# A four-layer graph network on one core: the preamble recorded in the plan, and the last six groups levelled, with all their steps through DRAM

## The chip, the core and the metric

The kernel runs on one core of a Trainium2 chip. The metric is device time in microseconds, from the first to the last instruction of the core; the time before is the median of three runs, 1416.56 us (1415.75 to 1422.14). The engines are named as in the profile: PE is TensorE (matmuls), PEld its weight loads, DVE VectorE, ACT ScalarE, POOL GpSimd, SP SyncE (here the issuer of most DMAs).

## The reference

`x` has 64 graphs of 256 nodes with 128 features, `adj` is one 256 x 256 matrix for all graphs, and everything is float32. Each of four layers adds its result to `x` and normalises over the features. Cut to what is computed:

```python
def layernorm(x): return (x - mean(x)) / sqrt(var(x) + 1e-5)        # over the 128 features

# layer 0: powers of adj, twice the same matrix; weight (128, 128, 7)
parts = [x, adj@x, adj@adj@x, adj@adj@adj@x, adj@x, adj@adj@x, adj@adj@adj@x]
x = layernorm(x + einsum('bnik,iok->bno', stack(parts), w0))
# layer 1
x = layernorm(x + adj @ (x @ w1) + b1)
# layer 2: A_hat = adj + I, d = rowsum(A_hat)**-0.5
x = layernorm(x + (d[:, None] * A_hat * d[None, :]) @ x @ W2.T + b2)
# layer 3: five gated steps with in_matrix = out_matrix = adj
h = x
for _ in range(5):
    m = adj @ h;  av = concat([m, m]);  u3 = h @ u3_w.T + u3_b
    z = sigmoid(av @ w3_w.T + w3_b + u3)
    r = sigmoid(av @ w4_w.T + w4_b + u3)
    hv = tanh(av @ w5_w.T + w5_b + (r * h) @ u5_w.T + u5_b)
    h = (1 - z) * h + z * hv
x = layernorm(x + h)
```

## The kernel before

Two graphs make a group: 2 x 256 nodes x 128 features lie as one 128 x 512 float32 tile, and 32 groups pass through the layers. The weights are folded in advance (`w34T` is the third gate weight less the fourth, so that `pr` serves first for r and then for z). A preamble makes the constants, in the program order in which it is written. Then each group is recorded as a list of operations, with an engine, a cost, what it reads and writes and a rank (the group's number); a list scheduler (`Plan.order`) settles the order of instructions of every engine and the buffer of every value. At most six groups are active.

The preamble:

```python
    a_nat = const.tile([P, T, N], F32, name="a_nat")
    nc.sync.dma_start(a_nat, adj.rearrange("(t p) m -> p t m", p=P))
    ...
    for mt in range(T):
        pt = bank(f"at_{mt}")
        for nt in range(T):
            nc.tensor.transpose(pt[:, nt * P:(nt + 1) * P], a_nat[:, nt, mt * P:(mt + 1) * P], ident)
        nc.vector.tensor_copy(aT[:, mt, :], pt[:, :N])
    ...                                   # aTp: the rows of aT in another order, by four DMAs
    for mt in range(T):
        pt = bank(f"apow_{mt}")
        for kt in range(T):
            mm(pt[:, :N], a_nat[:, kt, mt * P:(mt + 1) * P], aT[:, kt, :], kt == 0, kt == T - 1)
        nc.vector.tensor_copy(a2T[:, mt, :], pt[:, :N])
    ...                                   # anT: normalised adjacency, with deg, dinv (POOL) and ahat
    w0_raw = const.tile([P, C, K0], F32, name="w0_raw")
    nc.scalar.dma_start(w0_raw, w0)
    ...                                   # w1s, b1s, b2s
    w34 = halves("w3T", w3_w)
    nc.vector.tensor_sub(w34, w34, w4b)
    w4T = transposed("w4T", w4b)          # one TensorE transpose and one DVE copy each
    ...                                   # w34T, w5T, u3T, u5T; biases zb, rb, hb, two column DMAs each
```

A group's load, first propagation, and its five steps. `propagate` multiplies with the adjacency into `pmq`, `pm` or `pmg` and copies the result with ACT. A step needs `h` in node layout for the propagation and `hT` in feature layout for everything else. The first 30 groups get `h` from `hT` by a DVE transpose of 32 x 32 blocks, a store to DRAM and two rearranging reads (`packed`); the last two (TAIL = 2) by four TensorE transposes (`pth`) and an ACT copy.

```python
            x_ = self.val("x", "x")
            plan.add("SP", 450, 2700, g, lambda: nc.sync.dma_start(nat(x_), view(x, g)), [], [x_], self.load_gate)
            if g < HEAD:                                   # HEAD = 2
                xT = self.copied("xT", self.transposes("x", x_))
            else:
                xT = self.brought("xT", self.turned("x", x_, ...))     # DVE transpose (tx), DRAM, four reads
            qT = self.propagate("q", x_, a2)
            ...                                            # layers 0, 1 and 2
            if g < G - TAIL:
                hT = self.brought("hT", self.turned("h", h, ...))
                outs = by_block
            else:
                pT = self.transposes("h", h)
                ...
            for s in range(STEPS):
                m = self.propagate(f"g{s}", h, ats, ins, outs)
                pr = self.val("bank", f"pr{s}")
                self.product(pr, u3T, hT, True, False)
                self.product(pr, w4T, m, False, True)
                r = self.gate_(f"r{s}", pr, AF.Sigmoid, rb)
                rh = self.tensor(f"rh{s}", OP.mult, r, hT)
                ph = self.val("bank", f"ph{s}")
                self.product(ph, w5T, m, True, False)
                self.product(pr, w34T, m, False, True, shared=True)
                z = self.gate_(f"z{s}", pr, AF.Sigmoid, zb)
                self.product(ph, u5T, rh, False, True)
                hv = self.gate_(f"hv{s}", ph, AF.Tanh, hb)
                d = self.tensor(f"d{s}", OP.subtract, hv, hT)
                e = self.tensor(f"e{s}", OP.mult, z, d)
                hT = self.tensor(f"hT{s}", OP.add, hT, e)
                if g < G - TAIL:
                    if s < STEPS - 1:
                        h, ats, ins = self.packed(f"h{s}", hT), a1p, pair_of
                else:
                    pT = self.transposes(f"h{s}", hT)
                    if s < STEPS - 1:
                        h = self.copied(f"h{s}", pT)
            ...                                            # residual (s), statistics (st, mv, ve, rs), y, output
```

A float32 product of 512 columns shows as two TensorE passes in the profile (x2), a propagation as eight.

Of the kernel before, what the change touches and what calls it, by code (L numbers as in the profile page):

```python
# [13 lines left out]
P = 128  # L14
# [3 lines left out]
TAIL = 2  # L18
STEPS = 5
EPS = 1e-5  # L20
# [3 lines left out]
class Val:  # L24

# [16 lines left out]
class Plan:  # L42
# [29 lines left out]
    def order(self):  # L72
        free = {}
        pool = {k: [(0.0, i) for i in range(n)] for k, n in self.slots.items()}
        left = {op: len(op.deps) for op in self.ops}
        after = {op: [] for op in self.ops}
# [9 lines left out]
        while any(ready.values()):  # L86
            best = None
            for e, waiting in ready.items():
                t0 = free.get(e, 0.0)
                pick = None  # L90
                for at, op in waiting:
                    need = {}
                    for v in op.vals:
                        if v.slot is None:
                            need[v.kind] = need.get(v.kind, 0) + 1
                    short = False
                    for k, n in need.items():
                        if len(pool[k]) < n:
                            short = True
                            break  # L100
                        at = max(at, sorted(pool[k])[n - 1][0])
                    if short:
                        continue
                    key = (max(at, t0), op.rank, op.seq)
                    if pick is None or key < pick[0]:
                        pick = (key, op)
# [7 lines left out]
            for v in op.vals:  # L114
# [30 lines left out]
def kernel(  # L145
# [39 lines left out]
    prep = ctx.enter_context(tc.tile_pool(name="prep", bufs=2))  # L185
    setup = ExitStack()
    psum = setup.enter_context(tc.tile_pool(name="psum", bufs=BANKS, space=bass.MemoryType.PSUM))

    def bank(name):
        return psum.tile([P, 512], F32, tag="bank", name=name)  # L190

    def mm(o, lhsT, rhs, start, stop, shared=False):
        nc.tensor.matmul(o, lhsT, rhs, start=start, stop=stop, skip_group_check=shared)  # L193


    ident = const.tile([P, P], F32, name="ident")
    make_identity(nc, ident)
    a_nat = const.tile([P, T, N], F32, name="a_nat")
    nc.sync.dma_start(a_nat, adj.rearrange("(t p) m -> p t m", p=P))
# [4 lines left out]
    aT = const.tile([P, T, N], F32, name="aT")  # L204
    a2T = const.tile([P, T, N], F32, name="a2T")
    for mt in range(T):
        pt = bank(f"at_{mt}")
        for nt in range(T):
            nc.tensor.transpose(pt[:, nt * P:(nt + 1) * P], a_nat[:, nt, mt * P:(mt + 1) * P], ident)
        nc.vector.tensor_copy(aT[:, mt, :], pt[:, :N])  # L210

    aTp = const.tile([P, T, N], F32, name="aTp")
    for k in range(4):
        nc.sync.dma_start(aTp.rearrange("(i k) t n -> k i t n", k=4)[k], aT[32 * k:32 * (k + 1)])
    for mt in range(T):
        pt = bank(f"apow_{mt}")
        for kt in range(T):
            mm(pt[:, :N], a_nat[:, kt, mt * P:(mt + 1) * P], aT[:, kt, :], kt == 0, kt == T - 1)
        nc.vector.tensor_copy(a2T[:, mt, :], pt[:, :N])


    ahat = const.tile([P, T, N], F32, name="ahat")
    nc.vector.tensor_copy(ahat, a_nat)
    for t in range(T):
        diag = ahat[:, t, t * P:(t + 1) * P]
        nc.vector.tensor_add(diag, diag, ident)
    deg = const.tile([P, T], F32, name="deg")
    nc.vector.reduce_sum(deg, ahat, axis=AX.X)
    dinv = const.tile([P, T], F32, name="dinv")
    nc.gpsimd.tensor_tensor(dinv, deg, half[:, :T], op=OP.pow)  # L230
    for t in range(T):
        nc.vector.tensor_scalar(ahat[:, t, :], ahat[:, t, :], dinv[:, t:t + 1], None, op0=OP.mult)
    anT = const.tile([P, T, N], F32, name="anT")
    for mt in range(T):
        pt = bank(f"an_{mt}")
        for nt in range(T):
            nc.tensor.transpose(pt[:, nt * P:(nt + 1) * P], ahat[:, nt, mt * P:(mt + 1) * P], ident)
        nc.vector.tensor_scalar(anT[:, mt, :], pt[:, :N], dinv[:, mt:mt + 1], None, op0=OP.mult)
# [3 lines left out]
    w0_raw = const.tile([P, C, K0], F32, name="w0_raw")  # L242
    nc.scalar.dma_start(w0_raw, w0)

    w0s = const.tile([P, 4, C], F32, name="w0s")
    nc.vector.tensor_add(w0s[:, 0, :], w0_raw[:, :, 0], ident)
    for k in (1, 2, 3):
        nc.vector.tensor_add(w0s[:, k, :], w0_raw[:, :, k], w0_raw[:, :, k + 3])
    w1s = const.tile([P, C], F32, name="w1s")
    nc.scalar.dma_start(w1s, w1)  # L250
    b1s = const.tile([P, C], F32, name="b1s")
    nc.scalar.dma_start(b1s, bass.AP(tensor=b1.tensor, offset=b1.offset, ap=[[0, P], [1, C]]))
    b2s = const.tile([P, C], F32, name="b2s")
    nc.scalar.dma_start(b2s, bass.AP(tensor=b2.tensor, offset=b2.offset, ap=[[0, P], [1, C]]))

    def transposed(name, src):
        pt = bank(f"pt_{name}")
        nc.tensor.transpose(pt[:, :P], src, ident)
        t = const.tile([P, P], F32, name=name)
        nc.vector.tensor_copy(t, pt[:, :P])  # L260
        return t

    def loaded(name, src, shape):
        t = prep.tile(shape, F32, tag=f"raw{shape[1]}", name=f"raw_{name}")
        nc.scalar.dma_start(t, src)
        return t

    def halves(name, src):
        raw = loaded(name, src, [P, 2 * C])
        both = const.tile([P, C], F32, name=f"both_{name}")  # L270
        nc.vector.tensor_add(both, raw[:, :C], raw[:, C:])
        return both

    def bias_sum(name, a, b):
        raw = prep.tile([P, 2], F32, tag="rawb", name=f"raw_{name}")
        nc.scalar.dma_start(raw[:, 0:1], a.rearrange("(p o) -> p o", o=1))
        nc.scalar.dma_start(raw[:, 1:2], b.rearrange("(p o) -> p o", o=1))
        t = const.tile([P, 1], F32, name=name)
        nc.vector.tensor_add(t, raw[:, 0:1], raw[:, 1:2])
        return t  # L280

    w2T = transposed("w2T", loaded("w2T", w2, [P, C]))


    w4b = halves("w4T", w4_w)
    w34 = halves("w3T", w3_w)
    nc.vector.tensor_sub(w34, w34, w4b)
    w4T = transposed("w4T", w4b)
    w34T = transposed("w34T", w34)
    w5T = transposed("w5T", halves("w5T", w5_w))  # L290
    u3T = transposed("u3T", loaded("u3T", u3_w, [P, C]))
    u5T = transposed("u5T", loaded("u5T", u5_w, [P, C]))
    zb = bias_sum("zb", w3_b, u3_b)
    rb = bias_sum("rb", w4_b, u3_b)
    hb = bias_sum("hb", w5_b, u5_b)


    SHAPES = {"bank": [P, 512], "x": [P, 512], "w": [P, 512], "dram": [P, 512], "st": [P, Q * 6], "mv": [P, Q * 2],
              "ve": [P, Q], "rs": [P, Q]}
    slots = {"bank": BANKS, "x": ACTIVE + 3, "w": 58, "dram": 16, "st": 8, "mv": 8, "ve": 8, "rs": 8}  # L300
    plan = Plan(slots)
# [29 lines left out]
    class Group:  # L331
        def __init__(self, g):
            self.g, self.first, self.last = g, None, None
            self.gate = self.load_gate = ()

# [3 lines left out]
        def add(self, engine, cost, lag, run, reads=(), writes=()):  # L339
            after = () if self.first else self.gate  # L340
            op = plan.add(engine, cost, lag, self.g, run, reads, writes, after)
# [54 lines left out]
        def propagate(self, tag, h, aTs, ins=None, outs=None):  # L396
# [3 lines left out]
            def run():  # L400
                o, a = (outs or plain)(ps), ins or tile_of
                for b in range(NB):
                    for kt in range(T):
                        mm(o[b], a(h, b * T + kt), aTs[kt], kt == 0, kt == T - 1)

            self.pe(pe_cost(N, NB * T), run, [h], [ps])
# [49 lines left out]
        def product(self, ps, w, rhs, start, stop, shared=False):  # L456
            self.pe(pe_cost(512), lambda: mm(ps.ap, w, rhs.ap, start, stop, shared), [rhs], [ps])

        def gate_(self, name, ps, func, bias):
            t = self.val("w", name)  # L460
            self.act(lambda: nc.scalar.activation(t.ap, ps.ap, func, bias=bias, scale=1.0), [ps], [t],  # L461
# [3 lines left out]
        def tensor(self, name, op, a, b):  # L465
            t = self.val("w", name)
            self.dve(dve_cost(512), lambda: nc.vector.tensor_tensor(t.ap, a.ap, b.ap, op=op), [a, b], [t])  # L467
            return t

        def record(self):  # L470
# [10 lines left out]
            qT = self.propagate("q", x_, a2)  # L481
# [3 lines left out]
            for t in range(T):  # L485
# [3 lines left out]
                def first(p=p, t=t):  # L489
                    for b in range(NB):  # L490
                        o, n0 = p.ap[:, b * 2 * C:(b + 1) * 2 * C], b * N + t * P
                        mm(o, xT.ap[:, n0:n0 + P] if g < HEAD else by_node(xT)[:, b * T + t, :], w0s[:, 0:2, :], b == 0, True, shared=True)
                        mm(o, qT.ap[:, n0:n0 + P], w0s[:, 2:4, :], False, True, shared=True)
# [4 lines left out]
                self.pe(pe_cost(2 * C, 2 * NB), first, [xT, qT], [p])  # L498
                self.act(moved, [p], [v], act_cost(256))
            for t in range(T):  # L500

                def second(p=py[t], t=t):
                    for kt in range(T):
                        mm(four(p)[:, :, 0, :], aT[:, kt, t * P:(t + 1) * P], parts(v)[:, kt],
# [6 lines left out]
                self.pe(pe_cost(NB * C, T), second, [v], [py[t]])  # L511
# [4 lines left out]
            for tag, ats, w, bias in (("1", a1, w1s, b1s), ("2", an, w2T, b2s)):  # L516
                yb = self.val("w", "yb" + tag)

                def biased(yb=yb, y=y, bias=bias):
                    nc.gpsimd.tensor_tensor(nat(yb), nat(y), bias[:, None, :].to_broadcast([P, Q, C]),  # L520
                                            op=OP.add)

                self.add("POOL", 1290, 100, biased, [y], [yb])
# [3 lines left out]
                def weight(py=py, m=m, w=w):  # L527
                    for q in range(Q):
                        mm(py.ap[:, q * P:(q + 1) * P], m.ap[:, q * P:(q + 1) * P], w, True, True)

                self.pe(pe_cost(P, Q), weight, [m], [py])
# [4 lines left out]
            outs = None  # L536
            if g < G - TAIL:
# [96 lines left out]
```

## Time and profile before

| | |
|---|---|
| time, median of 3 | 1416.56 us (1415.75 to 1422.14) |
| span of the profiled run | 1415.3 us, 16464 instructions |
| granted TensorE clock, mean | 0.995 |
| PE / PEld / DVE / ACT / POOL busy | 97% / 65% / 68% / 36% / 16% |
| chain that ended last | PE 95%, DVE 2%, DMA 1%, ACT 1% |
| DMA traffic | 129.76 MB, 92 GB/s over the span |

The page gives busy time by engine, then 40 slices of the span, each digit a tenth of busy time, then the chain of work that ended last. Queries of the trace add timelines, waits and busy time by chosen stretch. A busy TensorE in it isn't TensorE at its peak, because its passes overlap and their ends are modelled: what is exact is when each starts. Idle time of an engine that isn't the bound costs nothing.

### The profile page before, as it was taken

The page shows a single profiled execution, that of the slowest core. Times are in us where ns is not written, and L with a number is a line of the kernel's source. Part 1 is how long each engine was busy: PE and PEld are TensorE (multiplying, and loading weights), DVE is VectorE, ACT ScalarE, POOL GpSimd, SP SyncE. Part 2 cuts the span into 40 slices and gives each one's busy share as a digit, 9 for nine tenths or more (in the row PEclk, how much of TensorE's full clock was granted, in tenths as well). Part 3 has the DMA queues.
Part 4 walks back from the last instruction along what each step waited for, and adds up shares of the span by engine and source line. Part 5 has one row for each costly group of instructions (what it writes and reads, how often), then busy time and mean ns, then how long its engine had stood idle before and what let it go on. Part 6 is the DMA issues. An engine that isn't in the chain of part 4 may idle for free.

```text
span 1415.3 us, 16464 instructions
## 1 busy us (share of the span) xinstructions
PE 1376.4 (97%) x5006; PEld 925.0 (65%) x5006; DVE 967.8 (68%) x2706; ACT 511.8 (36%) x812; POOL 224.5 (16%) x199
## 2 busy tenths in 40 slices
PE   5999999999999999999999999999999999999994
PEld 4866666667766676656666666676666766766552
DVE  3666577758775787857867666775777676676654
ACT  1233433343343323343333333334333344333442
POOL 0411011101210031201202111210121111121000
PEclk9999999999999999999999999999999999999998
DMA  5022343323333332324323333232433233322101
GB/s 169 16 60 80 92 128 111 95 76 105 105 104 91 100 108 76 111 82 135 98 82 104 97 100 114 88 110 75 118 104 98 82 112 90 97 82 67 53 23 30
DMA packets 245448, 129.76 MB, mean 92 GB/s; under 512 B 137968, under 2 KB 218224, under 8 KB 245360
## 3 DMA queue, kind: packets, MB, share of 16 engines
q1 hardware_dynamic: 243056, 127.46, 30.5%
q10 hardware_dynamic: 2304, 1.25, 0.4%
q8 instruction: 40, 0.66, 0.2%
q14 instruction: 48, 0.39, 0.1%
HBM read 64.95 MB, written 63.44 MB: 91 GB/s over the span
## 4 chain that ended last, share of the span: by engine, by line
PE 95%; DVE 2%; DMA 1%; ACT 1%; issue 0%; POOLq 0%; POOL 0%; SPq 0%; DVEq 0%; ACTq 0%
PE pr L193 29%; PE pmg L193 19%; PE ph L193 19%; PE py L193 16%; PE pm L193 8%; PE pmq L193 4%; DMA x<-in_x_dram 1%; PE pth L414 0%; DVE e L467 0%; DVE d L467 0%; DVE hT L467 0%; PE apow L193 0%; DVE y L390 0%; ACT hv L461 0%; DVE st L365 0%
## 5 line engine op out<-in xcount | busy, mean ns | idle before, releaser
L376 POOL TENSOR_TENSOR rs<-ve,half 128x4 f32<-128x4 f32 x128 | 134.1, 1050 | 1080.9 <-DVE ve L370 1076.2
L467 DVE TENSOR_TENSOR d<-hv,hT 128x512 f32<-128x512 f32 x160 | 112.6, 705 | 189.4 <-ACT hv L461 186.4
L467 DVE TENSOR_TENSOR rh<-r,hT 128x512 f32<-128x512 f32 x160 | 115.0, 719 | 166.7 <-ACT r L461 162.7
L193 PE MATMUL pmg<-aTp,h 128*128 128x256 f32 x960 | 225.0, 379 | 0.0
L193 PEld LDWEIGHTS pmg<-aTp,h 128*128 128x128 f32 x960 | 187.8, 196 | 42.8 <-issue 19.7
L357 ACT COPY mg<-pmg 128x512 f32<-128x512 f32 x160 | 93.8, 586 | 234.8 <-PE pmg L193 218.5
L461 ACT ACTIVATE z<-pr,zb 128x512 f32<-128x512 f32 x160 | 109.9, 688 | 168.9 <-PE pr L193 160.0
L390 DVE TENSOR_SCALAR y<-s,mv,rs 128x128 f32<-128x128 f32 x512 | 143.9, 345 | 36.7 <-POOL rs L376 36.3
L193 PE MATMUL pr<-mg,w4T 128*128 128x512 f32 x320 | 163.3, 593 | 1.4 <-ACT mg L357 1.4
L193 PE MATMUL pr<-mg,w34T 128*128 128x512 f32 x320 | 162.7, 594 | 1.7 <-ACT r L461 1.6
L193 PE MATMUL ph<-rh,u5T 128*128 128x512 f32 x320 | 162.2, 593 | 0.3 <-DVE rh L467 0.3
L193 PE MATMUL ph<-mg,w5T 128*128 128x512 f32 x320 | 162.4, 592 | 0.0
L193 PE MATMUL pr<-hT,u3T 128*128 128x512 f32 x320 | 161.5, 595 | 0.5 <-DVE hT L467 0.5
L461 ACT ACTIVATE r<-pr,rb 128x512 f32<-128x512 f32 x160 | 110.0, 688 | 128.5 <-PE pr L193 118.3
L461 ACT ACTIVATE hv<-ph,hb 128x512 f32<-128x512 f32 x160 | 110.0, 687 | 42.7 <-PE ph L193 41.5
L467 DVE TENSOR_TENSOR e<-z,d 128x512 f32<-128x512 f32 x160 | 111.7, 702 | 2.2
L467 DVE TENSOR_TENSOR hT<-hT,e 128x512 f32<-128x512 f32 x160 | 109.4, 687 | 2.4
L365 DVE BATCH_NORM_STATS2 st<-s 128x6 f32<-128x128 f32 x512 | 109.5, 277 | 0.7
L193 PEld LDWEIGHTS ph<-rh,u5T 128*128 128x128 f32 x320 | 60.5, 190 | 72.9 <-issue 62.0
L193 PEld LDWEIGHTS ph<-mg,w5T 128*128 128x128 f32 x320 | 60.5, 190 | 70.5 <-issue 54.8
L193 PEld LDWEIGHTS pr<-mg,w34T 128*128 128x128 f32 x320 | 59.5, 190 | 59.8 <-issue 51.7
L193 PEld LDWEIGHTS pr<-mg,w4T 128*128 128x128 f32 x320 | 60.0, 190 | 47.4 <-issue 42.1
(95 smaller groups left out, 1590.0 us busy)
## 6 DMA issues: line engine op xcount, KB each, us to landing
dh<-th SPq DMA_DIRECT2D x150, 256.0 KB, 2.0
h<-dh SPq DMA_DIRECT2D x240, 128.0 KB, 2.5
x<-in_x_dram SPq DMA_DIRECT2D x32, 256.0 KB, 3.2
out_dram<-y SPq DMA_DIRECT2D x32, 256.0 KB, 2.4
dx<-tx SPq DMA_DIRECT2D x30, 256.0 KB, 2.3
xT<-dx SPq DMA_DIRECT2D x120, 64.0 KB, 2.0
hT<-dh SPq DMA_DIRECT2D x120, 64.0 KB, 2.0
dn<-tn SPq DMA_DIRECT2D x30, 256.0 KB, 2.0
```

The source lines that it names most:

```text
L193: nc.tensor.matmul(o, lhsT, rhs, start=start, stop=stop, skip_group_check=shared)
L357: self.act(lambda: nc.scalar.copy(t.ap, ps.ap), [ps], [t])
L365: nc.vector.bn_stats(st.ap[:, q * 6:(q + 1) * 6], nat(s)[:, q, :])
L376: lambda: nc.gpsimd.tensor_tensor(rs.ap, ve.ap, half, op=OP.pow), [ve], [rs])
L390: nc.vector.tensor_scalar(nat(y)[:, q, :], nat(s)[:, q, :], mv.ap[:, 2 * q:2 * q + 1], rs.ap[:, q:q + 1], op0=OP.subtract, op1=OP.mult)
L461: self.act(lambda: nc.scalar.activation(t.ap, ps.ap, func, bias=bias, scale=1.0), [ps], [t], act_cost(512) + 100)
L467: self.dve(dve_cost(512), lambda: nc.vector.tensor_tensor(t.ap, a.ap, b.ap, op=op), [a, b], [t])
```

## The change

The preamble's work becomes operations of the plan, with ranks of their own, so that the scheduler weaves it into the first groups. A dummy activation makes ScalarE load its function table at the very start, and 24 transposes of the identity give TensorE early work. The transposes of the weights share two banks and two ACT copies; the six bias columns become one tile with one sum; w0 and the biases move to the SyncE queue. Loads of `x` for groups 2 to 7 now wait for that of the group two before.

In the last six groups (LEVEL) the rank no longer is the group's number, but rises with the group's own count of operations, so that a group that is behind goes first and they catch up with one another. The TensorE transposes in the steps are gone: all groups go through DRAM in every step. The last four groups (END) transpose once, after the last step, on TensorE, for the final residual; the others bring the last `hT` back through DRAM as before. Work slots go from 58 to 54.

The diff, cut (the rest renames constants into values of the plan):

```diff
-TAIL = 2
+LEVEL = 6
+END = 4
 STEPS = 5
+WARM = 24
...
-    slots = {"bank": BANKS, "x": ACTIVE + 3, "w": 58, "dram": 16, "st": 8, "mv": 8, "ve": 8, "rs": 8}
+    slots = {"bank": BANKS, "x": ACTIVE + 3, "w": 54, "dram": 16, "st": 8, "mv": 8, "ve": 8, "rs": 8}
...
+    early = constant("early", [P, Q])
+    pre(-9, "ACT", 1500, lambda: nc.scalar.activation(early.ap, half, AF.Sigmoid), [], [early])
+    warm = temp("warm")
+    def warmed():
+        for i in range(WARM):
+            nc.tensor.transpose(warm.ap[:, (i % 4) * P:(i % 4 + 1) * P], ident, ident)
+    pre(-9, "PE", 3000, warmed, [], [warm])
+    a_nat = load(-9, "SP", "a_nat", [P, T, N], adj.rearrange("(t p) m -> p t m", p=P))
...
+    pre(-8, "PE", 4 * 110, lambda: turn(p_at, a_nat), [a_nat], [p_at])
+    pre(-8, "DVE", dve_cost(512), lambda: nc.vector.tensor_copy(flat(aT), p_at.ap), [p_at], [aT])
+    pre(-8, "PE", pe_cost(N, 4), square, [a_nat, aT], [p_a2])
+    pre(-8, "ACT", act_cost(512), lambda: nc.scalar.copy(flat(a2T), p_a2.ap), [p_a2], [a2T])
+    w0_raw = load(0, "SP", "w0_raw", [P, C, K0], w0)
...
+    pre(1.5, "SP", 1800, spread, [aT], [aTp])
+    pre(0.3, "DVE", 1500, degree, [a_nat], [ahat, deg])
...
+    pre(0.4, "DVE", 220, lambda: nc.vector.tensor_sub(both["w34"].ap, both["w3"].ap, both["w4"].ap),
+        [both["w3"], both["w4"]], [both["w34"]])
...
+    w2T, u3T = transposed("w2u3T", raw["w2"], raw["u3"])
+    w4T, w34T, w5T, u5T = transposed("w435u5T", both["w4"], both["w34"], both["w5"], raw["u5"])
+    def biases():
+        for i, src in enumerate((w3_b, w4_b, w5_b, u3_b, u3_b, u5_b)):
+            nc.sync.dma_start(braw.ap[:, i:i + 1], src.rearrange("(p o) -> p o", o=1))
+    pre(2.5, "SP", 2200, biases, [], [braw])
+    pre(0.4, "DVE", 150, lambda: nc.vector.tensor_add(bsum.ap, braw.ap[:, :3], braw.ap[:, 3:]), [braw], [bsum])
...
-            op = plan.add(engine, cost, lag, self.g, run, reads, writes, after)
+            self.count += 1
+            rank = self.g
+            if self.g >= G - LEVEL:
+                rank = G - LEVEL + (self.g - G + LEVEL) / 10 + self.count / 100
+            op = plan.add(engine, cost, lag, rank, run, reads, writes, after)
...
-                if g < G - TAIL:
-                    if s < STEPS - 1:
-                        h, ats, ins = self.packed(f"h{s}", hT), a1p, pair_of
-                else:
-                    pT = self.transposes(f"h{s}", hT)
-                    if s < STEPS - 1:
-                        h = self.copied(f"h{s}", pT)
...
+                if s < STEPS - 1:
+                    hT = self.tensor(f"hT{s}", OP.add, hT, e)
+                    h, ats, ins = self.packed(f"h{s}", hT), aTp, pair_of
+            if g < G - END:
+                hT = self.tensor("hT", OP.add, hT, e)
+                hn = self.brought("hn", self.turned("n", hT, ...))
...
+            else:
+                hT = self.tensor("hT", OP.add, hT, e, ..., ...)     # written in block order
+                last = self.residual("3", self.transposes("h", hT), y)
...
             group.load_gate = (groups[g - ACTIVE - 2].last,)
+        elif g >= HEAD:
+            group.load_gate = (groups[g - HEAD].first,)
```

## The prediction

> **What bounds the kernel now.** I read the page's engine totals and its 40 slices first, to see whether one engine is the bound and where it isn't:
>
> ```profile
> PE 1376.4 (97%) x5006; PEld 925.0 (65%) x5006; DVE 967.8 (68%) x2706; ACT 511.8 (36%) x812; POOL 224.5 (16%) x199
> PE   5999999999999999999999999999999999999994
> ```
>
> TensorE (PE) is busy in every slice but the first and the last. Next, the busy time of each engine in chosen stretches (columns: stretch, its length, busy time of PE, weight load, DVE, ACT and POOL with counts, granted TensorE clock, DMA share, GB/s):
>
> ```profile
> 0.00:10.00 10.00, 1.09 (x4) 0.71 (x4) 1.65 (x6) 0.00 (x0) 0.70 (x6) 1.00 0.76 221
> 10.00:20.00 10.00, 4.47 (x14) 3.64 (x15) 8.21 (x21) 0.00 (x0) 0.71 (x1) 1.00 0.88 260
> 20.00:30.00 10.00, 7.42 (x35) 6.17 (x33) 2.00 (x9) 3.40 (x5) 0.00 (x0) 0.83 0.42 116
> 200.00:1200.00 1000.00, 999.33 (x3622) 672.25 (x3621) 710.73 (x1974) 371.47 (x590) 166.39 (x142) 1.00 0.34 100
> 1390.00:1400.00 10.00, 6.29 (x18) 3.55 (x16) 3.18 (x8) 2.52 (x4) 0.00 (x0) 0.83 0.09 26
> 1400.00:1416.00 16.00, 4.52 (x12) 1.77 (x12) 5.90 (x18) 2.09 (x4) 1.01 (x1) 0.78 0.06 17
> ```
>
> In the middle 1000 us TensorE stands still for 0.7 us. Time can be won there only by giving it less to do; otherwise it must come from the first 30 us or the last 40. So I read the timeline at both ends (start, duration, engine, line, operation, and in brackets the idle time before it with what ended it):
>
> ```profile
> 12.68 1.08 DVE L422 STREAM_TRANSPOSE tx<-x 128x512 f32<-128x512 f32 x1
> 15.06 0.75 DVE L210 COPY aT<-at 128x256 f32<-128x256 f32 x2
> 15.53 3.78 PE L193 MATMUL apow<-aT,a_nat 128*128 128x256 f32 x8 [8.91 <-DVE aT L210]
> 23.44 1.12 PE L414 MATMUL ptx<-ident,x 128*128 128x128 f32 x4 [0.38 <-DVE u5T L260]
> 27.61 1.89 PE L193 MATMUL pmq<-a2T,x 128*128 128x256 f32 x8
> ...
> 1383.50 0.66 PE L414 MATMUL pth<-ident,hT 128*128 128x128 f32 x4 [2.96 <-DVE hT L467]
> 1394.50 0.63 PE L414 MATMUL pth<-ident,hT 128*128 128x128 f32 x4 [3.11 <-DVE hT L467]
> 1396.32 3.08 PE L193 MATMUL pmg<-aT,h 128*128 128x256 f32 x8
> 1407.02 0.63 PE L414 MATMUL pth<-ident,hT 128*128 128x128 f32 x4 [3.05 <-DVE hT L467]
> ```
>
> Start: adj has landed and been transposed by 6.6, but DVE, in program order, first transposes x tiles whose loads are late, so aT is copied at 15.06; A squared follows, then all constants, and the first group begins at 23.44. The second group's first propagation, at 27.61, is the last that the start delays; from there TensorE is dense. Tail: three times TensorE waits about 3 us for a finished step of the only group left, and after the second the clock halves (3.08 for what takes 1.89).
>
> **What the Trainium skill says.** (1) "TensorE: Matmul & The Clock Gate", Part 1: the array runs at half clock until it has been busy for about 3.4 us, and falls back after such a time idle. The trace agrees: eight 256-column passes take 3.78 at 15.53 and 3.08 after the 3.11 idle, but 1.89 elsewhere. (2) The same page, Part 4: transposes do not count as busy in that sense. That bears on the 24 warming transposes; no transpose here was a long run from cold, so the trace doesn't decide. (3) "ScalarE: Activation LUTs", "What ACT_TABLE_LOAD costs": about 1.28 us; the trace has 1.28 at 23.47, beside ptx. (4) "DMA: Bandwidth & Descriptors", "Latency and other measured facts": some 2 us is the fixed cost of a DMA. The table of DMA issues (last column: us to landing) agrees:
>
> ```profile
> dh<-th SPq DMA_DIRECT2D x150, 256.0 KB, 2.0
> h<-dh SPq DMA_DIRECT2D x240, 128.0 KB, 2.5
> ```
>
> **The change, part by part.** The order of instructions in the changed program is known from building it; the durations below are from the rows before.
>
> *Start.* SyncE issues adj, w0, x0 and x1 first, later groups' x later; ScalarE loads its table and issues the weights. adj was issued at 0.74 and took 4.7: 5.4. The 24 transposes begin once the identity is there (1.3) at 0.22 each cold (four took 1.09 at 5.53), 0.11 warm: done between 4.5 and 6.6. DVE runs its copy and sums for the degree first (0.43 + 0.46 + 0.68 from 5.4), then the aT copy (0.68): about 7.8. TensorE's order has the transposes of x0 and x1 ahead of the square; x loads took 6.0 (median of the first two) after issue, so x1 lands near 8.5 and the square starts near 8.8. It takes 1.7 warm, 3.5 cold; the ACT copy 0.6 plus 0.2: a2T at 11.3 to 13. First group's propagation 1.7: done at 13 to 14.8. The next thing in TensorE's queue is the transposes of w34 and w5, and w34 stands on DVE behind the bias sum. The six bias columns wait in the SyncE queue, each for the DMA eight places ahead: the last is issued near 11 and lands 2.0 to 2.3 later, so w34 is ready near 13.9. Hence the second group's propagation starts at 14.4 (warm) to 15.5 (cold) instead of 27.61: **12.1 to 13.2 us less; I take 12.3**, for late DMAs.
>
> *TensorE work.* The two tail groups had 2 x (1 + 5) batches of four transposes; now four end groups have one each. A batch moves the next instruction by 0.43 (1302.15 to 1302.59): 12 - 4 = 8 batches, **3.4 us less** on the bound engine. Propagations through aTp cost what those through aT did (379 ns a pass in both rows). Ten more stores, 16 more reads and eight more DVE transposes of 0.7 lie beside TensorE at 68% DVE and 34% DMA.
>
> *Tail.* Starts of TensorE rows after 1300 compared with undisturbed spacing (0.86 for a 512-column product, 1.73 for a propagation, 0.43 for four transposes): the three hT waits with the 0.16 that pipelining hides 9.6, half clock 2.5, two mg waits 1.7, three smaller waits at 1320, 1339 and 1378 3.3, and after the last transposes 7.9. **25 us of loss.**
>
> After: a lone step takes 11.5 today (1384.86 to 1396.32). From the last ph to the next propagation that is 4.5 (1380.4 to 1384.86); through DRAM it is hv 0.9, d, e, hT and transpose 4 x 0.72, store 0.3 + 2.0, reads 0.6 + 2.5: 9.2. So a step takes 16.2, and TensorE works 6.0 in it (1.73 + 5 x 0.86). Three groups fill it (18), two don't (12). The changed order keeps six groups level and ends with propagations of groups 28, 30, 29, 31, 30, 31. I walked that end by hand with these durations: dense through 28; then DVE is the limit (13 operations, 9.5 us, ahead of the next hT): 1.9 lost; waits for mg 3 x 0.85; before the transposes of 30 3.1; the last group alone 3 more; then hv to output 11.5 as today (1403.8 to 1415.3). From the last dense row 44.6 us with 25.8 of work: 18.8 lost, and I add 2 for half clock after the 3 us gap. **21 against 25: 4 us less.**
>
> Sum: 12.3 + 3.4 + 4 = 19.7. 1416.56 - 19.7 = **1397 us**, 1.4% less.
>
> **Rivals.** *A: a late DMA takes DVE's place at the start.* For: DVE and SyncE work in order, and bias columns and weights stand ahead of the x tiles, on waits of 3 to 5 us each. Against: the traffic of the first 10 us gets less. If w34 comes 5 us later: 1402. *B: DRAM latency opens the tail.* For: 9.2 against 4.5 in each step. Against: three groups hide it, and only one step is left alone where there were two. If two steps stay alone, 9 us are lost: 1406. *C: levelling fills the tail*, and only the final chain and one gap stay, some 14 lost: 1390. *D: 54 work slots instead of 58 stall the middle.* Against: 0.7 us idle in 1000 and the plan orders by slots; half a per cent would be 7 us: 1404.
>
> **Range and chances.** Start 9 to 14, work 3.4, tail -2 to 10 give 10 to 27, hardly ever both ends together: 1389 to 1404. 2% is 28.3 us (1388.2) and needs C with a perfect start: 10%. Slower by 2% would need a stall in the middle of 48 us: 1%.
>
> **What would show it.** Right: the second pmq at 14 to 16; a table load before 3 us; eight fewer batches of transposes; the middle still above 99.8%; TensorE losing 18 to 23 us after its last dense stretch. Wrong: gaps before the bias sum or w435u5T beyond 15 us (A), pmg waiting for h at the end (B), a middle with waits for slots (D). Warming transposes that stay 0.22 apart and a square of 3.5 would settle the page's remark.

## The result, and the profile after

The changed kernel takes 1395.51 us (median of four runs, 1394.63 to 1397.23), beside 1418.99 us for the kernel before on the same occasions (1415.75 to 1422.14). The ratio is 0.9836, with a 95% interval of 0.9806 to 0.9866. The profiled run has a span of 1394.3 us, against 1415.3 before: 21.0 us less. The prediction said 1397 us, in a range of 1389 to 1404.

First the engine totals of the page after:

```profile
PE 1374.0 (99%) x4998; PEld 926.1 (66%) x4998; DVE 972.9 (70%) x2701; ACT 508.0 (36%) x807; POOL 230.8 (17%) x199
```

TensorE's busy time hardly changed, because the warming transposes are counted in it: what went away is idle time at the ends. The stretches of the changed kernel show it (stretch, length, busy time of PE, weight load, DVE, ACT and POOL with counts, clock, DMA share, GB/s):

```profile
0.00:10.00 10.00, 6.35 (x32) 5.81 (x32) 4.24 (x13) 1.49 (x2) 1.42 (x7) 0.98 0.61 182
10.00:20.00 10.00, 9.70 (x45) 8.34 (x46) 4.05 (x9) 3.60 (x7) 0.00 (x0) 0.85 0.50 141
200.00:1200.00 1000.00, 999.31 (x3660) 677.80 (x3659) 716.62 (x2024) 368.31 (x586) 176.96 (x148) 1.00 0.33 98
1370.00:1380.00 10.00, 6.27 (x18) 3.56 (x17) 5.21 (x17) 1.96 (x3) 1.01 (x1) 0.83 0.16 42
1380.00:1396.00 16.00, 3.88 (x11) 1.42 (x9) 5.89 (x18) 2.06 (x3) 1.01 (x1) 0.66 0.11 33
```

The middle is as dense as before (999.31 against 999.33 of 1000 us), and the last 24 us look as they did: one stretch with a lone wait and a halved clock, and one final chain. Before, two lone waits stood ahead of that chain, the second with the halved clock behind it. Now the timeline at both ends, in order of start:

```profile
1.36 5.19 PE L228 MATMUL warm<-ident 128*128 128x128 f32 x24 [1.36 <-POOL ident masks.py:199]
6.39 0.60 PE L240 MATMUL p_at<-ident,a_nat 128*128 128x128 f32 x4
9.18 0.73 PE L461 MATMUL ptx<-ident,x 128*128 128x128 f32 x4 [2.19 <-DMA x<-in_x_dram]
10.28 1.11 PE L461 MATMUL ptx<-ident,x 128*128 128x128 f32 x4 [0.36 <-DMA x<-in_x_dram]
11.18 2.81 PE L190 MATMUL p_a<-aT,a_nat 128*128 128x256 f32 x8
15.45 0.16 DVE L341 TENSOR_TENSOR bsum<-braw 128x3 f32<-128x3 f32 x1 [4.19 <-DMA braw<-in_L_gnn_u_b_dram]
16.50 0.49 PE L324 MATMUL p_w435u5T<-ident,both_w 128*128 128x128 f32 x3
16.94 1.89 PE L190 MATMUL pmq<-a2T,x 128*128 128x256 f32 x8
...
1360.15 1.12 PE L190 MATMUL pr<-mg,w435u5T 128*128 128x512 f32 x2 [0.68 <-ACT mg L404]
1374.30 0.63 PE L461 MATMUL pth<-ident,hT 128*128 128x128 f32 x4 [3.05 <-DVE hT L515]
1374.77 3.44 PE L190 MATMUL pmg<-aTp,h 128*128 128x256 f32 x8
1385.72 1.11 PE L461 MATMUL pth<-ident,hT 128*128 128x128 f32 x4 [2.96 <-DVE hT L515]
```

**Start.** The second group's first propagation begins at 16.94 instead of 27.61: 10.7 us less. aT is ready at 7.7, but the square (p_a) waits until 11.18, because the transposes of x0 and x1 stand ahead of it in TensorE's queue and those tiles land only just before 9.18 and 10.28. The bias sum comes at 15.45, but does not delay TensorE: the first group's propagation, begun at 14.67, keeps it busy until 16.4, and the transposes of w34 follow at 16.50 without a wait.

**Tail.** With the same count as in the prediction (starts of TensorE rows after 1300 us against undisturbed spacing, plus what follows the last transposes) TensorE loses 10.7 + 8.1 = 18.8 us instead of 25. Two waits for hT are left instead of three, one of them followed by half clock.

**Work.** pth now has 16 transposes instead of 48, which is the eight batches of 0.43 us.

10.7 + 3.4 + 6.2 = 20.3 of the 21.0 us between the two spans.

### The profile page after: what moved, and what is told of

It reads as the page before. It is cut to its first block, busy times and chain, and to the rows that moved or that the text cites. A ratio compares the mean times of both kernels' runs of the same rounds, so it can differ in the third digit from the quotient of the medians.

```text
span 1394.3 us, 16512 instructions
## 1 busy us (share of the span) xinstructions
PE 1374.0 (99%) x4998; PEld 926.1 (66%) x4998; DVE 972.9 (70%) x2701; ACT 508.0 (36%) x807; POOL 230.8 (17%) x199
## 4 chain that ended last, share of the span: by engine, by line
PE 95%; DVE 3%; issue 1%; DMA 1%; POOL 0%; ACT 0%; SPq 0%; POOLq 0%; DVEq 0%
PE pr L190 29%; PE pmg L190 19%; PE ph L190 19%; PE py L190 16%; PE pm L190 8%; PE pmq L190 4%; DVE y L437 1%; DMA x<-in_x_dram 1%; DVE st L412 1%; POOL rs L423 0%; DVE e L515 0%; DVE hT L515 0%; DVE s L428 0%; DVE d L515 0%; PE pth L461 0%
## 5 line engine op out<-in xcount | busy, mean ns | idle before, releaser
L190 PE MATMUL pr<-mg,w435u5T 128*128 128x512 f32 x640 | 321.0, 593 | 2.0 <-ACT mg L404 2.0
L190 PEld LDWEIGHTS pr<-mg,w435u5T 128*128 128x128 f32 x640 | 119.9, 190 | 103.3 <-issue 93.0
L508 ACT ACTIVATE z<-pr,bsum 128x512 f32<-128x512 f32 x160 | 110.0, 688 | 155.8 <-PE pr L190 141.8
L190 PE MATMUL ph<-rh,w435u5T 128*128 128x512 f32 x320 | 162.0, 593 | 0.3 <-DVE rh L515 0.3
L190 PE MATMUL ph<-mg,w435u5T 128*128 128x512 f32 x320 | 162.3, 592 | 0.0
L190 PE MATMUL pr<-hT,w2u3T 128*128 128x512 f32 x320 | 161.3, 593 | 0.4 <-DVE hT L515 0.4
L508 ACT ACTIVATE r<-pr,bsum 128x512 f32<-128x512 f32 x160 | 110.0, 688 | 136.2 <-PE pr L190 134.0
L508 ACT ACTIVATE hv<-ph,bsum 128x512 f32<-128x512 f32 x160 | 110.0, 687 | 53.8 <-PE ph L190 53.3
L190 PEld LDWEIGHTS ph<-mg,w435u5T 128*128 128x128 f32 x320 | 60.5, 190 | 69.5 <-issue 54.3
L490 DVE STREAM_TRANSPOSE th<-hT 128x512 f32<-128x512 f32 x128 | 90.2, 706 | 1.7
```

Of the source, the lines that this page charges most:

```text
L490: self.dve(dve_cost(512), lambda: nc.vector.transpose(turn.ap.rearrange("p (u j t) -> p u t j", t=T, j=32), src.ap.rearrange("p (u t i) -> ...
```

## The experiments

My theory: TensorE is dense in the middle, so the change is worth what the two ends give up, and they add. Rivals: DVE or DMA is what really paces the middle and gives an earlier start back later; DRAM round trips are hidden by six active groups whether they are levelled or not; the warm clock is a part of the gain. Ratios are to the kernel before.

### The two halves apart

`pre_only` has the new preamble and the old tail; `tail_only` has the old preamble and the new tail.

```diff
# pre_only, on the changed kernel
-                rank = G - LEVEL + (self.g - G + LEVEL) / 10 + self.count / 100
+TAIL = 2      # and the steps of the last two groups as in the kernel before
# tail_only, on the kernel before
-TAIL = 2
+LEVEL = 6
+END = 4       # and ranks, steps and last residual as in the changed kernel
```

> The new preamble with the old tail (rank = group number, the last two groups' steps through TensorE transposes). Theory, that the two halves add: the second group's first propagation starts within 0.5 us of the 16.94 of the changed kernel, the loss of TensorE after 1300 us is that of before (25 us), the span is 1415.3 - 10.7 = 1404.6 us. Rival, that an earlier start only moves waits to the end (DVE or DMA is what really paces the middle): the span stays above 1410 us.

> The old preamble with the new tail (levelled ranks, all steps through DRAM, four end groups with one batch of transposes each). Theory: the first group starts at 23.4 us as before, eight batches of transposes fewer give 3.4 us, the tail loses 19 us instead of 25: span near 1405.5 us. Rival, that the tail's gain came only because groups were shifted by the early start: span above 1410 us.

`pre_only`: 1406.49 us, ratio 0.9913 (0.9892 to 0.9934), span 1405.4; second propagation at 16.54 us, 26.8 us lost at the end. `tail_only`: 1407.17 us, ratio 0.9923 (0.9906 to 0.994), span 1405.6. The product of the ratios is 0.9837; the changed kernel has 0.9836. The halves add, as far as the intervals (some 3 us either way for each half) can show. The profiles are sharper: from the second propagation to the end the old tail takes 1387.7 us behind the old preamble and 1388.9 behind the new one, the new tail 1377.3 and 1377.4. So neither gain is given back in the middle.

### Levelling taken away

```diff
-            if self.g >= G - LEVEL:
-                rank = G - LEVEL + (self.g - G + LEVEL) / 10 + self.count / 100
```

> The changed kernel with rank = group number for all groups; all steps still through DRAM. Theory, that levelling is what hides the DRAM round trips at the end: the last group has two lone steps of about 16 us with 6 us of TensorE work each, so 6 to 10 us more than the changed kernel, near 1402 us. Rival, that DRAM round trips are hidden anyway by the six active groups: within 2 us of the changed kernel.

It takes 1413.4 us, ratio 0.9965 (0.9955 to 0.9976): 18 us more than the changed kernel, where I expected 6 to 10. TensorE's timeline of this run has waits of about 3 us and more for a group's step in several places, not only in the last two steps:

```profile
1344.28 1.12 PE L190 MATMUL pr<-hT,w2u3T 128*128 128x512 f32 x2 [2.96 <-DVE hT L513]
1365.80 1.13 PE L190 MATMUL pr<-hT,w2u3T 128*128 128x512 f32 x2 [2.96 <-DVE hT L513]
1366.79 3.48 PE L190 MATMUL pmg<-aTp,h 128*128 128x256 f32 x8
1385.23 2.07 PE L190 MATMUL pr<-hT,w2u3T 128*128 128x512 f32 x2 [3.86 <-DVE hT L513]
1390.47 3.75 PE L190 MATMUL pmg<-aTp,h 128*128 128x256 f32 x8 [3.16 <-DMA h<-dh]
```

With groups in order, only six propagations are left from 1340 us on, and too little work of other groups stands beside a step to fill its wait. Most of the loss is waiting: the four waits above and the last one before pth (2.95) make 15.9 us, against 3.05 + 2.96 = 6.0 in the changed kernel. Half clock adds less: two propagations take 3.48 and 3.75 us instead of 1.89, against one in the changed kernel. Not every gap of 3 us brings it: after the one at 1344.28 the next sixteen passes take 3.62 us, which is full clock. `no_level` against `pre_only` (1413.4 against 1406.49) also shows what sending the tail through DRAM costs by itself: 6.9 us more (6.5 from the second propagation to the end of the two profiles), although eight batches of transposes are gone. Levelling more than pays for that. So six active groups alone don't hide the DRAM round trips; with the levelled ranks they do, all but the last one.

### The warming transposes taken away

```diff
-WARM = 24
-    pre(-9, "PE", 3000, warmed, [], [warm])
+WARM = 0
```

> The changed kernel without the 24 warming transposes. Theory: they bring next to nothing, because TensorE then stands still for 2.2 us until x of the first group lands and the clock is lost again before the square; the transposes of adj run at half speed, 0.22 us apart, but start near 3.8 us, and the second group's propagation starts within 1 us of 16.94; time within 0.1%. Rival: the warm clock carries over, and without it the second propagation starts 2 us or more later.

1395.01 us, ratio 0.9837 (0.9815 to 0.9858): the same time. TensorE's timeline:

```profile
3.87 1.09 PE L239 MATMUL p_at<-ident,a_nat 128*128 128x128 f32 x4 [3.87 <-DMA a_nat<-in_adj_dram]
8.48 2.21 PE L460 MATMUL ptx<-ident,x 128*128 128x128 f32 x8 [3.53 <-DMA x<-in_x_dram]
16.40 1.89 PE L190 MATMUL pmq<-a2T,x 128*128 128x256 f32 x8
```

The four transposes of adj take 1.09 cold where they took 0.60 behind the warming ones, so the 24 transposes do warm the clock. But they also hold adj's transposes back from 3.87 to 6.39, and the 2 to 3.5 us of waiting for x follow either way. They bring no time that these runs show. They may do so in some executions: in four of the five other profiles with these 24 transposes the square ran at full clock (1.89 us, against 2.97 here), and the second propagation started at 14.59 to 15.05 us. Whether that is their doing is not shown, as there is one profile without them.

### What bounds the start

`square_first` makes the transposes of x0 and x1 depend on the square. `start_best` also issues x0 and x1 ahead of w0, and lets the bias columns and the weights' transposes of later layers start only after the second propagation.

```diff
+                self.last.deps.add(squared)              # ptx of groups 0 and 1 after p_a
# start_best, besides
-    w0_raw = load(0, "SP", "w0_raw", [P, C, K0], w0)
+    w0_raw = load(1.2, "SP", "w0_raw", [P, C, K0], w0)
+            if g == 1:
+                for op in late:                          # biases, p_w2u3T, p_w435u5T
+                    op.deps.add(qT.writer)
```

> The changed kernel with the square of adj ahead of the transposes of x0 and x1 in TensorE's queue (those now depend on it). Theory, that the start has two bounds one behind the other: the square starts near 7.8 us at full clock instead of 11.2, but the transposes of w34 and w5 still wait for the bias sum (15.45 us) and stand ahead of the second group's propagation, so that one starts between 15.9 and 16.9 and the time stays within 0.1% of the changed kernel. Rival, that x0 and x1 alone hold the start back: the second propagation starts near 13.5 us, 3 us less.

> The same, and x0 and x1 issued ahead of w0, and the bias columns and the weights' transposes for later layers only after the second group's first propagation. Theory: both bounds are gone, the second propagation starts at 12 to 13.5 us instead of 16.94, about 4 us less, near 1391 us. Rival, that later loads (biases, aTp, x of group 2) then come too late and give it back: within 1 us of the changed kernel.

`square_first`: 1394.95 us, ratio 0.9841 (0.9822 to 0.986). `start_best`: 1395.91 us, ratio 0.985 (0.9828 to 0.9871). Neither is faster. TensorE's timeline of the first, then of the second:

```profile
7.26 1.99 PE L190 MATMUL p_a<-aT,a_nat 128*128 128x256 f32 x8 [1.30 <-DVE aT L247]
10.61 0.33 PE L324 MATMUL p_w2u3T<-ident,raw_u 128*128 128x128 f32 x1 [1.25 <-DMA raw_u<-in_L_gnn_u_w_dram]
14.58 1.89 PE L190 MATMUL pmq<-a2T,x 128*128 128x256 f32 x8
```

```profile
11.55 1.12 PE L240 MATMUL p_an<-ident,ahat 128*128 128x128 f32 x4 [2.34 <-DVE ahat L292]
13.31 2.88 PE L190 MATMUL pmq<-a2T,x 128*128 128x256 f32 x8
16.47 1.89 PE L190 MATMUL pmq<-a2T,x 128*128 128x256 f32 x8
```

The square does start early and warm. Then one bound follows another. In `square_first` a weight DMA (1.25 us) and the bias sum (13.34 in that run, 0.3 us) are next; the second propagation comes at 14.58, earlier than the 15.9 to 16.9 that I expected. In `start_best` the normalised adjacency's transposes wait on DVE for `ahat`, which stands behind w0's sums, and these wait for w0 until 9.96. My expectation of 12 to 13.5 us failed on that third bound, and on the clock, which was lost in that wait (the first propagation takes 2.88 us instead of 1.89).

Two things blur this. First, the start varies between profiles: the five other kernels that share the changed kernel's preamble unaltered start the second propagation at 16.54 (`pre_only`), 15.05 (`no_level`), 14.63 (`last_chip`), 14.59 (`gap_busy`) and 14.86 us (`chip2`), against 16.94. Most of this is the clock during the square. In `pre_only` and `chip2` the transposes of x1 start at the same time, 9.53 and 9.54 us. The square of the first, then of the second:

```profile
10.39 3.20 PE L191 MATMUL p_a<-aT,a_nat 128*128 128x256 f32 x8
10.03 1.89 PE L191 MATMUL p_a<-aT,a_nat 128*128 128x256 f32 x8
```

From start to start, the x1 transposes take 0.86 against 0.49 us and the square 3.04 against 1.73: 1.68 us, the whole difference between 16.54 and 14.86. The changed kernel's own profile has 2.31 us more than `last_chip`: x1 is 1.0 us later, half clock makes the other 1.3. Likewise `start_best` and `both_best` (below) have the same start, with `ahat` transposed at 11.55 and 11.52, but the second propagation at 16.47 and 14.78. Why the clock is kept in some executions and not in others stays open: `last_chip` kept it over a wait of 2.00 us for x0, `pre_only` lost it after waits of 1.44 and 0.45. The bias sum, at 13.68 to 15.45 in the six profiles, holds TensorE up by 0.2 us in `no_level` and not at all in the others.

Second, a new order at the start is a new order everywhere. The middle of `start_best`, by stretches:

```profile
200.00:1200.00 1000.00, 998.12 (x3669) 680.12 (x3669) 723.28 (x2030) 364.48 (x581) 178.09 (x150) 1.00 0.33 98
```

TensorE idles 1.9 us there instead of 0.7; counted by starts, 2.5 us more are lost between 1000 and 1200 us than in the changed kernel. `square_first` idles as much there (998.24 busy), so its earlier start does not reach the end.

### The last gap: its wait and its clock

`last_chip` gives the last group its state for the last step by TensorE transposes; `chip2` does it for the last two groups. `gap_busy` leaves everything as it is and puts 14 transposes of the identity behind the last ph of group 30.

```diff
# last_chip (CHIP = 1) and chip2 (CHIP = 2)
+                if g >= G - CHIP and s == STEPS - 2:
+                    hq = self.tensor("hq", OP.add, hT, e, ..., ...)          # in block order
+                    hT = self.tensor(f"hT{s}", OP.add, hT, e)
+                    h, ats, ins = self.copied("hc", self.transposes("hc", hq)), aT, None
# gap_busy
+                if g == G - 2 and s == STEPS - 1:
+                    self.pe(1500, filled, [ph], [fill])                      # 14 transposes of ident
```

> The changed kernel, but the last group gets its state for the last step by TensorE transposes and an ACT copy instead of through DRAM (one DVE operation and one batch of transposes more). Theory, that one DRAM round trip is still exposed at the end: the last propagation follows the ph of group 30 at once instead of 3.7 us later, the clock does not fall to half there (2.4 us); 4 to 5 us less, near 1391 us. Rival, that the gap is the wait for hT of group 30 and the order behind it: within 1 us of the changed kernel.

> The changed kernel with 14 transposes of the identity (1.5 us) behind the last ph of group 30, in the 3 us in which TensorE waits for that group's hT. Theory, that the fall to half clock after this gap is a cost of its own (2.4 us) and that transposes count as activity: the last propagation takes 1.9 us instead of 3.4, the span is about 1.5 to 2.4 us less after the same start, and the wait before pth is 1.5 us. Rival, that transposes don't count: the propagation still takes 3.1 us or more.

> As last_chip, but the last two groups get their state for the last step by TensorE transposes. Theory, that only one round trip was exposed, and that the two groups' stagger is lost when both take the short way: no better than last_chip, and up to 4 us more. Rival, that a second round trip was still costing time: 1 us or more below last_chip.

`last_chip`: 1390.32 us, ratio 0.9807 (0.9789 to 0.9825), the fastest version but for `chip2`, which is level with it (1390.39 us, 0.9801, 0.9783 to 0.9818): shortening a second round trip brings nothing more. `gap_busy`: 1392.0 us, ratio 0.9817 (0.9795 to 0.9839). TensorE's timeline of `last_chip`, then of `gap_busy`:

```profile
1367.56 1.02 PE L191 MATMUL ph<-rh,w435u5T 128*128 128x512 f32 x2
1368.42 1.89 PE L191 MATMUL pmg<-aT,hc 128*128 128x256 f32 x8
1379.86 0.78 PE L462 MATMUL pth<-ident,hT 128*128 128x128 f32 x4 [3.95 <-DVE hT L516]
```

```profile
1368.73 1.69 PE L604 MATMUL fill<-ident 128*128 128x128 f32 x14
1371.94 0.63 PE L461 MATMUL pth<-ident,hT 128*128 128x128 f32 x4 [1.52 <-DVE hT L515]
1372.41 1.90 PE L190 MATMUL pmg<-aTp,h 128*128 128x256 f32 x8
```

In `last_chip` the last propagation follows ph at once, and the loss at the end is 14.4 us instead of 18.8. From the second propagation to the end its profile is 3.7 us shorter; the rest of its lead over the changed kernel's profile is an earlier start (14.63). In `gap_busy` the same wait for hT lasts, filled half with work that computes nothing, and the propagation takes 1.90 instead of 3.44. By median it gains 3.5 us; its profile also starts earlier (14.59 against 16.94), so of its 4.2 us shorter span 1.85 belong to the gap. From the propagation to the next product it is 2.57 us instead of 4.11. So half clock costs 1.5 us here, not 2.4: my 2.4 held 0.8 of waiting for mg, which stays. The clock is thus a cost of its own beside the wait.

`both_best`, the start of `start_best` with the tail of `last_chip`:

> Start and tail of the two kernels before together. Theory, that the two ends add, because TensorE is dense between them: 8 to 9 us less than the changed kernel, near 1387 us. Rival, that only one of the two gains arrives: 1390 us or more.

1392.43 us, ratio 0.9822 (0.9803 to 0.984). The sum that I expected did not come: it is slower than `last_chip` by 2.1 us. Its start is no earlier (14.78 against 14.63), and its middle idles 1.9 us in 1000 instead of 0.7.

## Why the prediction was right

- **The bound and the form of the sum.** Right: the middle stayed at 999.3 of 1000 us, and the halves apart have ratios whose product is that of both.
- **Start, 12.1 to 13.2 us.** 10.7 in the changed kernel's profile, 11.1 to 13.0 in five others with the same preamble. The first waits were as worked out: x1, then the square. The last was not: w34 was ready at 15.8 instead of 13.9, but TensorE was busy until 16.4, so the bias sum bounded nothing. Two terms were too small in the changed kernel's own profile: x1 landed at 10.2 instead of 8.5, and the x1 transposes and the square ran mostly at half clock, which cost 1.3 us. So the sign that was named, a second pmq at 14 to 16 us, failed in this profile (16.94) and in `pre_only` (16.54), and held in the other four.
- **Warm or cold.** The prediction left it open whether transposes warm the clock. They do here: four transposes took 0.60 us after 24 others and 1.09 without them, and 14 kept the clock up over the last gap. The Trainium skill says in "TensorE: Matmul & The Clock Gate", Part 4, that the full rate does not engage for transposes; for the float32 transposes of this kernel these measurements decide against it. The median time is the same without the 24. In the changed kernel's own profile the clock was lost again while TensorE waited for x.
- **TensorE work, 3.4 us.** Right: 32 transposes fewer.
- **Tail, 21 us of loss.** 18.8: mis-sized by 2 us. The wait of 1.9 us behind 13 DVE operations did not appear (no idle time of TensorE from 1300 to 1358 us); the three waits for mg came (0.83 each), and so did the last gap (3.05, predicted 3.1), with 1.5 of half clock behind it instead of 2. In the prediction's account of the kernel before, the 2.5 of half clock held 0.8 of a wait for mg that was counted again among the mg waits; by starts the total still comes to some 25.
- **Rivals.** A came by its sign (a bias sum after 15 us) and cost nothing, as TensorE was still busy. B was real but covered by levelling: through DRAM without it costs 6.9 us more than the old tail. C needed the last round trip gone, which `last_chip` shows at 1390 us. D did not happen.

The tail's excess of 2.2 us and the start's shortfall of 1.6 us nearly cancel. That the total fits so closely is in part luck: with the clock kept in the square, as in four of the six profiles, the start alone would have gained some 1.3 us more.

## What to carry to other kernels

When one engine is dense in the middle, price a change by what each end loses, from the starts of that engine's instructions, and test the ends apart: if the ratios multiply to the whole, nothing is given back. Here levelling the last groups paid because a step's round trip was longer than the work of the groups still active, and the last lone step was best kept on chip. At the start, moving one load or one product forward only uncovered the next wait in an engine's fixed order, so follow every queue to its end before expecting microseconds, and see at which clock TensorE ran between the waits. A product that comes after others on the same engine can be late without costing anything: look at whether the engine was free.

## What had not been expected

- Levelling was worth 18 us (1413.4 against 1395.5 us), where 6 to 10 were estimated: without it five long waits stand in the tail instead of two, and two propagations run at half clock instead of one.
- Filling an idle gap with transposes of the identity is worth 1.85 us at the end (the last propagation takes 1.90 instead of 3.44 us). At the start, where another gap follows, the medians show no gain.
- The start of one and the same preamble varies by 2.4 us between profiles (14.59 to 16.94 us for the second propagation), up to 1.7 us of it by the clock alone, while the middle repeats to 0.1 us; a start read from one profile should carry that much doubt.
